# FFN tokens rounded to fp8 ahead of their transposition in a convolution, FFT and FFN block

## The chip, the cores and the metric

The kernel runs on one core of one Trainium2 chip. Times are device microseconds (us) of one execution. The core's engines are TensorE (PE, with its weight loads listed apart as PEld), VectorE (DVE), ScalarE (ACT), GpSimd (POOL) and SyncE (SP), which issues the loads and stores of the loop. The number that counts is the median time of the runs.

## The reference, cut to what matters

The input is 32 images of 56 x 56 pixels with 96 channels. Each image goes through three stages:

- a layer norm over channels, a linear map to 192 channels, a 3 x 3 convolution back to 96, silu, and the input added;
- a token mixer: layer norm, a linear map to 192 with relu, a Fourier transform over the 3136 tokens, a pointwise complex gate, the inverse transform and a linear map back to 96, added to the tokens;
- a feed-forward network (FFN): layer norm, then two linear layers (96 to 384 and back) whose factors are rounded to fp8 (5 exponent bits, 2 mantissa bits) and whose sums are rounded to fp16, with a relu between them, added to the tokens.

The change lies in the third stage. Its core in the reference:

```python
q_mul = lambda x: _float_quantize(x, 5, 2)
q_acc = lambda x: _float_quantize(x, 5, 10)
def _qlinear(x, W, b):
    y = q_acc(jnp.einsum('bsk,nk->bsn', q_mul(x), q_mul(W)))
    return q_acc(y + q_mul(b))
h = jax.nn.relu(_qlinear(x, W1, b1))
y = _qlinear(h, W2, b2)
...
t = t + ffn(_ln_t(t))
```

So the normalised tokens are rounded to fp8 before the first product.

## The kernel before, in words

An image's 3136 tokens lie as 112 partitions by 28 token columns (`N1`, `N2`) of 96 channels. The token columns are handled in 7 groups of 4 (`NG`, `G4`); the statistics and the convolution take chunks of 8, 8, 8 and 4 columns (`LN_CHUNKS`).

The convolution's input is made by products with a constant matrix (`image`, L153), its sums by the products of `conv` (L164, into `cv`); `to_tokens` (L196) transposes its result back. The mixer takes groups through `to_channels` (kind `n2`), `product_a` (L209, `ph`), `transform_a` (L218, `pa`), then a store of `u` to `da` in DRAM and a load of `at`, which turns the tokens round. `forward` (L233, `px`) does the second half of the transform from `at`; the gate follows on ScalarE and VectorE; `product_w2` (L272 and L276, `pg`) and `inverse` (L286, `pe`) lead to a second round trip through DRAM (`de`, then `y`), and `transform_out` (L294, `py`) ends the mixer.

The FFN of a group runs in these steps. `normal` (L479 to L488) makes the tokens `xn` from `t` on VectorE, one `tensor_scalar` for each token column with mean and reciprocal deviation as pointer operands; its output is f32, in a slot of the tag `xn` with two slots, which one load of image 0 shares (L362). `ffn_start` calls `ffn_tokens` (L297), which calls `to_channels` (L141): four TensorE transposes against the f32 identity (L146) put channels on the partitions, in the one PSUM buffer of the tag `tp`, which the mixer's `n2` transposes share. ScalarE's copy to `n3t` (L300) moves them out of PSUM and rounds them to fp8. `ffn_in` (L305, `pf`) multiplies by the first weights, three times a group, with an fp16 copy on ScalarE (L307). `ffn_relu` (L315, L316) works on VectorE, and `ffn_out` (L322, `po`) does twelve products a group with `hq` as weights. Over the 32 images the FFN has 224 groups and 896 transposes of `xn`.

The order of the work: `plan` gives each step of each image a due time by hand, in units of which an image has 8; images overlap by these times, so that the convolution of a coming image, the mixer and the FFN of earlier ones mix. `normal` is due at 0.7 and 0.55 before its group's FFN time, `ffn_start` at 0.35 before it, then three `ffn_first` and `ffn_middle`, `ffn_second` and `ffn_end`:

```python
put(at - 0.7, normal, g, 0)
put(at - 0.55, normal, g, 2)
put(at - 0.35, ffn_start, g)
```

`run` traces the steps in that order. The program framework then schedules the instructions itself, by priority and an estimate of time that it keeps as it goes (`schedule_with_timeline_sim=True`, L848), sets the semaphores, and assigns buffers. An engine's final order can therefore differ from the traced one within a short distance: products of other steps stand between the transposes of one group in places.[...]

At the start, `make_identity` (L89) builds the f32 identity on GpSimd, and a setup section prepares weights on VectorE and TensorE (L617, L675 and L719 are instructions of it), while the first tokens are loaded.

Of the kernel before, what the change touches and what calls it, by code (L numbers as in the profile page):

```python
# [38 lines left out]
F32 = mybir.dt.float32  # L39
F16 = mybir.dt.float16  # L40
F8 = mybir.dt.float8e5
AF = mybir.ActivationFunctionType
ALU = mybir.AluOpType
AX = mybir.AxisListType

C = 96
HW = 56
N = HW * HW
N1, N2 = 112, 28
# [9 lines left out]
G4 = 4  # L59
# [21 lines left out]
def hybrid_kernel(ctx: ExitStack, tc: tile.TileContext, x, par, spar, w_in, conv_w, w1, w2, fw1, fb1, fw2, fb2, fa, fb, ib, ia, rows6, out):  # L81
    nc = tc.nc
    nb = x.shape[0]

    const = ctx.enter_context(tc.tile_pool(name="const", bufs=1))


    ident = const.tile([128, 128], F32, name="ident")
    make_identity(nc, ident)  # L89
    mhalf = const.tile([N1, N2], F32, name="mhalf")  # L90
    nc.gpsimd.memset(mhalf, -0.5)

# [26 lines left out]
    xnp = ctx.enter_context(tc.tile_pool(name="xnp", bufs=2))  # L119
# [21 lines left out]
    def to_channels(xs, b, g, kind):  # L141

        rows = xs.shape[2]
        ps = psum.tile([rows, G4, N1], F32, tag="tp", name=f"tp_{kind}_{b}_{g}")
        for j in range(G4):
            nc.tensor.transpose(ps[:, j, :], xs[:, j, :], ident[:N1, :N1])  # L146
        return ps

    def image(xa, n, b, j0):
# [49 lines left out]
    def channels(xs, b, g):  # L199
        ps = to_channels(xs, b, g, "n2")  # L200
        n2t = w3.tile([C + 1, G4, N1], F32, tag="n2t", name=f"n2t_{b}_{g}")
        nc.scalar.copy(n2t, ps)
        return n2t
# [93 lines left out]
    def ffn_tokens(xs, b, g):  # L297
        ps = to_channels(xs, b, g, "n3")
        n3t = work.tile([C, G4 * N1], F8, tag="n3t", name=f"n3t_{b}_{g}")
        nc.scalar.copy(n3t, ps.rearrange("c j p -> c (j p)"), saturate=False)  # L300
        return n3t
# [177 lines left out]
    def normal(im, g, j):  # L479

        i = g // 2
        if j == 0:
            im.xc[g] = xnp.tile([N1, G4, C], F32, tag="xn", name=f"xn_{im.b}_{g}")
        mu, _, rs = im.norm[i]
        xc = im.xc[g]
        for j in (j, j + 1):
            at = g % 2 * G4 + j
            nc.vector.tensor_scalar(xc[:, j], im.t[i][:, at, :C], mu[:, at : at + 1], rs[:, at : at + 1], ALU.subtract, ALU.mult)  # L488

    def ffn_start(im, g):  # L490
        im.held["n3", g] = ffn_tokens(im.xc.pop(g), im.b, g)
# [27 lines left out]
    def plan(b):  # L519
# [27 lines left out]
        for g in range(NG):  # L547
            at = FIRST + g
            put(at - 0.35, tokens_a, g)
            for j2 in range(2):  # L550
                put(at + 0.15 + 0.6 * j2, forth, g, j2)
                put(at + 0.42 + 0.58 * j2, forth_a, g, j2)
            put(at + 1.2, store_a, g)
            at = BACK + g
            put(max(BACK - 0.6, at - 2.9), fetch_y, g)
            put(at, back, g)
            put(at + 0.15, back_end, g)
            at = FFN + g
# [3 lines that stand above are left out]
            for k in range(3):  # L562
                put(at + 0.28 * k, ffn_first, g, k)
                put(at + 0.28 * k + 0.17, ffn_middle, g, k)
            put(at + 1.0, ffn_second, g)
            put(at + 1.15, ffn_end, g)
            put(at + 1.5, store, g)
# [35 lines left out]
    with tc.tile_pool(name="setup", bufs=1) as sp, tc.tile_pool(  # L603
        name="setup_ps", bufs=2, space=bass.MemoryType.PSUM
# [15 lines left out]
        for g in range(2):  # L620
            ps = spp.tile([128, 512], F32, tag="ps", name=f"ps_wt{g}")
# [6 lines left out]
        for k in range(9):  # L628
            ps = spp.tile([128, 512], F32, tag="ps", name=f"ps_we{k}")
# [29 lines left out]
        for g in range(2):  # L659
            nc.vector.tensor_scalar(w1s[:, g, :C], w1s[:, g, :C], s1[:, g : g + 1], None, ALU.mult)  # L660
            nc.vector.tensor_copy(w1s[:, g, C : C + 1], o1[:, g : g + 1])
            ps = spp.tile([128, 512], F32, tag="ps", name=f"ps_w1{g}")
            nc.tensor.transpose(ps[: C + 1, :C], w1s[:, g, :], ident[:C, :C])
            nc.vector.tensor_copy(w1a[:, g * C : (g + 1) * C], ps[: C + 1, :C])
        ps = spp.tile([128, 512], F32, tag="ps", name="ps_w1c")
# [12 lines left out]
        for g in range(2):  # L678
            ps = spp.tile([128, 512], F32, tag="ps", name=f"ps_w2{g}")
# [6 lines left out]
        ps = spp.tile([128, 512], F32, tag="ps", name="ps_o2")  # L686
# [17 lines left out]
        for k in range(3):  # L704
            ps = spp.tile([128, 512], F32, tag="ps", name=f"ps_f1{k}")
            nc.tensor.transpose(ps[:C, :128], f1[:, k, :], ident)
            nc.vector.tensor_copy(w1q[:, k * 128 : (k + 1) * 128], ps[:C, :128], saturate=False)
            ps = spp.tile([128, 512], F32, tag="ps", name=f"ps_f2{k}")
# [143 lines left out]
```

## Time and profile before

| what | us |
|---|---|
| median of 3 runs | 3248.47 |
| lowest and highest of them | 3239.42, 3249.1 |
| profiled execution, its own time | 3247.36 |
| its span, first to last instruction | 3245.6 |
| TensorE busy | 3167.5 |
| TensorE weight loads busy | 2737.2 |
| VectorE busy | 2529.4 |
| ScalarE busy | 2196.2 |
| GpSimd busy | 598.2 |

The profile is one execution recorded by the hardware. An instruction group is given by its line, engine and operation, with output and inputs by name, then the tile as partitions by elements and type. For TensorE, `112*96 112x112` means 112 rows and 96 columns of weights, and 112 partitions by 112 elements streamed past them. After the count stand busy us and the mean ns of one, then the idle time before the group and what ended it. A wait line gives who waited for what, us in total, times, and the longest one. In a timeline each line is a start, a length, an engine and what ran, several like instructions merged into one line; an entry in square brackets is the idle time before it. The granted TensorE clock averaged 0.986 of full speed over the execution. The program spans stretches at the start and the end where only one or two images are at work; between them, images follow each other in a steady rhythm.

### The profile page before, as it was taken

Reading aid. Unit: us, or ns where it says so; the run is one execution under the profiler, and the core shown is the slowest. Engines: PE = TensorE matmul, PEld = TensorE weight load, DVE = VectorE, ACT = ScalarE, POOL = GpSimd, SP = SyncE. Lnnn points to the kernel's source line nnn. Section 1 sums busy time; section 2 is a strip of 40 time slices with the busy share of each in tenths; the row PEclk is TensorE's granted clock in tenths of the full one; section 3 lists DMA queues with packets and bytes.
Section 4 is the critical chain, followed back from the end, with each engine's and each line's share of the span. In section 5 each row is a group of like instructions: output and inputs, shape, how many; then the busy total and the mean of one; then the engine's idle time right before and its main releaser. Section 6 shows DMA issues by size and latency. Waiting matters only on the chain.

```text
span 3245.6 us, 66513 instructions
## 1 busy us (share of the span) xinstructions
PE 3167.5 (98%) x23701; PEld 2737.2 (84%) x23701; DVE 2529.4 (78%) x7829; ACT 2196.2 (68%) x5232; POOL 598.2 (18%) x397
## 2 busy tenths in 40 slices
PE   7999999999999999999999999999999999999997
PEld 6888888888888888888888888888888888888875
DVE  5557878877877877877877887878787878787777
ACT  2556676766776676766676766667667667767676
POOL 1211212111212111212121121111121112121111
PEclk8999999999999999999999999999999999999997
DMA  4343344343344433344333344333344333443341
GB/s 109 94 116 103 93 122 122 111 115 101 104 122 117 115 109 108 106 118 120 108 103 106 109 127 122 101 109 105 109 127 117 108 109 95 120 124 97 103 118 56
DMA packets 334551, 355.43 MB, mean 110 GB/s; under 512 B 129305, under 2 KB 287401, under 8 KB 333993
## 3 DMA queue, kind: packets, MB, share of 16 engines
q1 hardware_dynamic: 332210, 349.01, 38.6%
q8 instruction: 187, 3.06, 0.4%
q10 hardware_dynamic: 2008, 2.17, 0.2%
q14 instruction: 146, 1.19, 0.1%
HBM read 196.93 MB, written 154.14 MB: 108 GB/s over the span
## 4 chain that ended last, share of the span: by engine, by line
PE 87%; DMA 7%; DVE 3%; ACT 1%; issue 1%; SPq 0%; POOL 0%; ACTq 0%; DVEq 0%; POOLq 0%
PE cv L164 21%; PE px L233 9%; PE ph L209 9%; PE pa L218 8%; PE im L153 7%; PE tp_n L146 5%; PE pg L276 5%; PE pe L286 5%; PE pg L272 5%; PE py L294 4%; PE pf L305 4%; PE po L322 4%; DMA de<-es 2%; PE st L196 2%; DMA at<-da 2%; DMA y<-de 1%
## 5 line engine op out<-in xcount | busy, mean ns | idle before, releaser
L164 PE MATMUL cv<-img,wv 97*96 97x224 f32 (+1 forms) x4608 | 874.7, 330 | 0.2
L164 PEld LDWEIGHTS cv<-img,wv 97*96 97x96 f32 x4608 | 671.3, 164 | 101.0 <-issue 16.4
L138 POOL TENSOR_TENSOR rs_c<-var_c,mhalf 112x8 f32<-112x8 f32 (+1 forms) x128 | 198.3, 1549 | 1404.5 <-DVE var_c L136 1039.0
L307 ACT CAST h<-pf 128x448 f16<-128x448 f32 x672 | 362.2, 539 | 87.2 <-PE pf L305 86.4
L138 POOL TENSOR_TENSOR rs_b<-var_b,mhalf 112x8 f32<-112x8 f32 (+1 forms) x128 | 193.9, 1515 | 1194.7 <-DVE var_a L136 592.8
L233 PEld LDWEIGHTS px<-fb_sb,at 112*64 112x64 f32 (+1 forms) x3584 | 329.7, 165 | 94.7 <-issue 42.0
L212 ACT ACTIVATE h<-ph,rs_b 112x192 f32<-112x192 f32 x896 | 330.0, 424 | 105.7 <-PE ph L209 102.6
L233 PE MATMUL px<-fb_sb,at 112*64 112x112 f32 (+3 forms) x3584 | 378.2, 273 | 21.7 <-DMA at<-da 19.3
L209 PE MATMUL ph<-w1a,n2t 97*112 97x192 f32 x1792 | 380.2, 329 | 3.3 <-DVE sv L252 2.0
L218 PE MATMUL pa<-h,fa_sb 112*112 112x384 f32 x896 | 366.7, 491 | 0.3 <-DVE t L398 0.3
L315 DVE TENSOR_SCALAR h<-h,b1q 128x448 f16<-128x448 f16 x658 | 216.4, 329 | 178.1 <-ACT h L307 170.4
L153 PE MATMUL im<-rows_sb,xa 112*97 112x168 f32 x1792 | 333.4, 312 | 11.3 <-DVE xa L372 10.1
L209 PEld LDWEIGHTS ph<-w1a,n2t 97*112 97x112 f32 x1792 | 288.9, 177 | 32.1 <-DVE sv L252 2.6
L249 DVE SCALAR_TENSOR_TENSOR sv<-px,spar_sb,av 128x224 f32<-128x224 f32 (+2 forms) x352 | 153.9, 437 | 183.3 <-ACT av L240 180.7
L153 PEld LDWEIGHTS im<-rows_sb,xa 112*97 112x97 f32 x1792 | 262.9, 167 | 25.1 <-DVE xa L372 10.1
L219 ACT COPY u<-pa 112x384 f32<-112x384 f32 x448 | 216.2, 482 | 80.7 <-PE pa L218 76.3
L316 DVE CAST hq<-h 128x448 fp8e5<-128x448 f16 x672 | 259.2, 386 | 11.7 <-ACT h L313 6.7
L305 PE MATMUL pf<-n3t,w1q 96*128 96x448 fp8e5 x672 | 243.1, 362 | 7.4 <-ACT h L307 6.2
L276 PE MATMUL pg<-w2x,gt 128*112 128x96 f32 (+1 forms) x1792 | 245.3, 260 | 0.0
L322 PEld LDWEIGHTS <-hq 128*112 128x112 fp8e5 x2688 | 198.5, 135 | 51.7 <-DVE hq L316 16.9
L276 PEld LDWEIGHTS pg<-w2x,gt 128*112 128x112 f32 (+1 forms) x1792 | 239.8, 178 | 1.0
L488 DVE TENSOR_SCALAR xn<-t,st_c,rs_c 112x96 f32<-112x96 f32 x896 | 231.7, 324 | 10.1 <-POOL rs_c L138 7.3
(115 smaller groups left out, 6121.7 us busy)
## 6 DMA issues: line engine op xcount, KB each, us to landing
da<-u SPq DMA_DIRECT2D x224, 336.0 KB, 2.9
at<-da SPq DMA_DIRECT2D x224, 336.0 KB, 4.8
de<-es SPq DMA_DIRECT2D x448, 84.0 KB, 2.5
y<-de SPq DMA_DIRECT2D x224, 168.0 KB, 3.0
out<-o SPq DMA_DIRECT2D x224, 168.0 KB, 2.6
xl<-in_x SPq DMA_DIRECT2D x96, 336.0 KB, 3.5
x<-in_x SPq DMA_DIRECT2D x96, 336.0 KB, 4.0
xl<-in_x SPq DMA_DIRECT2D x32, 168.0 KB, 2.3
```

The costliest lines, as they stand in the source:

```text
L138: nc.gpsimd.tensor_tensor(rs, var, mhalf[:, :n], ALU.pow)
L153: nc.tensor.matmul(ps[:, j], xa[:, j, :], rows6_sb, start=True, stop=True)
L164: nc.tensor.matmul(ps[:, at], wv[:, k, dx, :], cols, start=(dx == 0), stop=(dx == 2))
L209: nc.tensor.matmul(ph[:, j, :], n2t[:, 2 * j2 + j, :], w1a, start=True, stop=True)
L212: nc.scalar.activation(h[:, j], ph[:, j], AF.Relu, scale=rs[:, 2 * j2 + j : 2 * j2 + j + 1])
L218: nc.tensor.matmul(pa, fa_sb, h, start=True, stop=True)
L233: nc.tensor.matmul(px[rows, j], lhs, fb_sb[:, first(p) : first(p + 1)], start=True, stop=True)
L276: nc.tensor.matmul(pg[:, half, j, :], lhs, w2x, start=False, stop=True, skip_group_check=True)
L305: nc.tensor.matmul(pf, w1q[:, k * 128 : (k + 1) * 128], n3t, start=True, stop=True)
L307: nc.scalar.copy(h1, pf)
L316: nc.vector.tensor_copy(hq[:, k, :], h2, saturate=False)
L322: nc.tensor.matmul(po[:, j, :], hq[:, k, j * N1 : (j + 1) * N1], w2q[:, k, :], start=(k == 0), stop=(k == 2))
```

## The change

The tokens are written as fp8 by `normal`, and the four transposes of a group are ordinary products of these fp8 tokens (as weights) with an fp8 identity. The result in PSUM is f32 as before, with values that are already rounded, and ScalarE's copy to `n3t` stays. The fp8 identity is made once at the start by VectorE from the f32 one. The mixer's transposes (`n2`) and the slots of the tags stay. Line numbers move by 2 from L90 on and by 5 from L147 on.

```diff
     ident = const.tile([128, 128], F32, name="ident")
     make_identity(nc, ident)
+    ident8 = const.tile([N1, N1], F8, name="ident8")
+    nc.vector.tensor_copy(ident8, ident[:N1, :N1], saturate=False)
...
         for j in range(G4):
-            nc.tensor.transpose(ps[:, j, :], xs[:, j, :], ident[:N1, :N1])
+            if xs.dtype == F8:
+                nc.tensor.matmul(ps[:, j, :], xs[:, j, :], ident8, start=True, stop=True)
+            else:
+                nc.tensor.transpose(ps[:, j, :], xs[:, j, :], ident[:N1, :N1])
         return ps
...
         if j == 0:
-            im.xc[g] = xnp.tile([N1, G4, C], F32, tag="xn", name=f"xn_{im.b}_{g}")
+            im.xc[g] = xnp.tile([N1, G4, C], F8, tag="xn", name=f"xn_{im.b}_{g}")
...
-            nc.vector.tensor_scalar(xc[:, j], im.t[i][:, at, :C], mu[:, at : at + 1], rs[:, at : at + 1], ALU.subtract, ALU.mult)
+            nc.vector.tensor_scalar(xc[:, j], im.t[i][:, at, :C], mu[:, at : at + 1], rs[:, at : at + 1], ALU.subtract, ALU.mult, saturate=False)
```

## The prediction

> **What bounds the kernel now.** I read the page's busy times and chain first, to name the engine, and then left the start and the end of the run aside and asked for the busy time and TensorE's waits of the stretch from 340 to 3140 us, in which one image takes the place of another every 97.8 us.
>
> ```profile
> PE 3167.5 (98%) x23701; PEld 2737.2 (84%) x23701; DVE 2529.4 (78%) x7829; ACT 2196.2 (68%) x5232; POOL 598.2 (18%) x397
> ...
> PE 87%; DMA 7%; DVE 3%; ACT 1%; issue 1%; SPq 0%; POOL 0%; ACTq 0%; DVEq 0%; POOLq 0%
> ```
>
> ```profile
> 340.00:3140.00 2800.00, 2773.16 (x21101) 2410.28 (x21100) 2235.73 (x6929) 1954.13 (x4673) 525.46 (x338) 1.00 0.40 111
> ```
>
> ```profile
> PE px L233 <- DMA at<-da: 16.9, 25, 2.7
> PE py L294 <- DMA y<-de: 5.8, 12, 1.3
> ```
>
> The second fence is the stretch (busy us of TensorE, its weight loads, VectorE, ScalarE, GpSimd; clock; DMA share); the third holds its two largest waits of TensorE (us in total, times, longest). TensorE is busy 2773 of 2800 us, at the full clock, and waits for other engines hardly at all: once an image for the transposed forward spectrum, less for the inverse one. But overlapping products make a busy share a poor measure, so the question is how densely they follow one another. A product's own duration says little there[...]; the distance from one start to the next is what it takes from TensorE.
>
> The groups of products by shape, then stretches of TensorE's timeline (start us, us, what):
>
> ```profile
> L305 PE MATMUL pf<-n3t,w1q 96*128 96x448 fp8e5 x672 | 243.1, 362 | 7.4 <-ACT h L307 6.2 <-DVE xn L488 0.6 <-ACT n3t L300 0.2
> L322 PE MATMUL po<-w2q,hq 128*112 128x96 fp8e5 x2688 | 215.7, 217 | 5.1 <-DVE hq L316 5.0
> L146 PE MATMUL tp_n<-ident,xn 112*96 112x112 f32 x896 | 152.7, 265 | 1.2 <-DVE xn L488 1.1
> ```
>
> ```profile
> 1600.63 0.92 PE L164 MATMUL cv<-img,wv 97*96 97x224 f32 x4
> 1601.39 0.81 PE L209 MATMUL ph<-w1a,n2t 97*112 97x192 f32 x4
> 1602.04 0.45 PE L153 MATMUL im<-rows_sb,xa 112*97 112x168 f32 x2
> ```
>
> ```profile
> 1615.10 0.67 PE L322 MATMUL po<-w2q,hq 128*112 128x96 fp8e5 x10
> 1615.61 0.87 PE L209 MATMUL ph<-w1a,n2t 97*112 97x192 f32 x4
> 1616.31 0.26 PE L164 MATMUL cv<-img,wv 97*96 97x112 f32 x1
> ```
>
> ```profile
> 1642.06 0.55 PE L146 MATMUL tp_n<-ident,xn 112*96 112x112 f32 x4
> 1642.44 0.73 PE L164 MATMUL cv<-img,wv 97*96 97x224 f32 x3
> ```
>
> ```profile
> 1619.89 0.26 PE L146 MATMUL tp_n<-ident,xn 112*96 112x112 f32 x1
> 1619.99 0.61 PE L233 MATMUL px<-fb_sb,at 112*128 112x112 f32 x4
> 1620.44 0.26 PE L146 MATMUL tp_n<-ident,xn 112*96 112x112 f32 x1
> 1620.53 0.39 PE L233 MATMUL px<-fb_sb,at 112*128 112x112 f32 x2
> ```
>
> Read the starts. Four f32 transposes of xn take 1642.44 - 1642.06 = 0.38 us, 95 ns each. Ten fp8 products of 96 columns take 1615.61 - 1615.10 = 0.51 us, 51 ns each. And the same four ph products take 0.65 us behind f32 work (1601.39 to 1602.04) but 0.70 us behind fp8 work (1615.61 to 1616.31): a short fp8 product hides too little of the f32 weight load that follows. The last fence shows the framework's scheduler laying other products between the four transposes of a group.
>
> [...]pf with 448 columns starts its follower 191 to 193 ns later[...]. For f32 the trace shows double: 323 ns for pa's 384 columns.[...]
>
> **The change, part by part.**
>
> *Transposes, the only part on TensorE.* 896 products (32 images x 7 groups x 4) go from f32 to fp8, both the moving identity (112 columns) and the weights (96). Now: median distance 96 ns. After: [...]51 measured on po, whose weights are larger and whose columns are fewer. I take 50. Gain 896 x 46 ns = 41.2 us, all on the path, since TensorE is the bound.
>
> *What the switch back costs.* Behind a po product, an f32 one with a load of 96 or 97 columns ends 42 ns later than behind f32 (im 186 against 143 ns from the end before; cv 231 against 189), one of 112 columns 55 ns later (ph 219 against 163). An fp8 transpose covers some 7 ns more than po (112 columns for 96): 35 and 48 ns; for 128 columns another 13 by the same step, so 61. How often it is paid depends on the runs. In TensorE's order the 896 transposes form 375 runs: 147 of one, 39 of two, 85 of three, 104 of four. 69 are followed by an fp8 product, which I set at nothing, 116 by an f32 one with 96 or 97 columns, 110 with 112, 80 with 128 (px, as in the last fence). Sum: 116 x 35 + 110 x 48 + 80 x 61 = 14.2 us. Net 27.0 us. The bounds: nothing is paid (41 us gained), or every transpose is followed by f32 work (896 x 47 = 42 us lost, gain nil).
>
> *VectorE, L488.* It writes the normalised tokens as fp8: the same 896 instructions.
>
> ```profile
> L488 DVE TENSOR_SCALAR xn<-t,st_c,rs_c x896: 299/324/339, 241.4 to 3220.9; 112x96 f32<-112x96 f32 x180
> ```
>
> ```profile
> 26.20 0.19 DVE L719 CAST b<-b 112x96 fp8e5<-112x96 f32 x1
> ```
>
> The first is its line (min/median/max ns), the second a cast of the same 96 elements from f32 to fp8 in the setup, 0.19 us: no slower than f32 to f32 of that size (L617 0.26 with one pointer operand). From L617 to L675, a like operation on 192 elements in 0.31 us, 96 more elements cost 0.05 us.[...] I take nothing. VectorE is idle for 3246 - 2529 = 716 us and TensorE waits 1.1 us for xn[...].
>
> *The rest.* The identity's cast at the start: one VectorE instruction, about 0.2 us by L719, in front of statistics that wait 3.6 us for the first load; nothing. The eviction L300 reads the same f32 PSUM tile and rounds values that are fp8 already: same cost. No DMA, no pool depth and no semaphore in the loop is added; the xn slots keep their f32 size, since a load of image 0 shares them. The eviction may begin about 0.18 us sooner after the group's first transpose (four times 46 ns), which helps.
>
> *What is late next.* With some 0.8 us less TensorE work an image, TensorE comes sooner to px and py, whose data makes a round trip through DRAM that doesn't shrink. These waits can grow by what is saved inside the round trip. The page's DMA part gives the landings as 2.9 us for da, 4.8 for at, 2.5 for de and 3.0 for y, together 13.2 of the 97.8 us of an image; the same share of 0.8 us is 0.11 us an image, 3.5 us in all. Forecast gain 27.0 - 3.5 = 23.5 us.
>
> The profiled execution took 3247.4 us (span 3245.6), the median of the runs is 3248.5: the two are 0.03% apart. 3247.4 - 23.5 = 3224 us.
>
> **The rivals.**
>
> *The gain comes whole.* If the scheduler keeps the groups of four together, 224 runs remain: 224 x 47 = 10.5 us of switches, gain 31; if fp8 neighbours hide those too, 41. That gives 3206 to 3217 us. For it: the order is made anew from changed instructions. Against it: the interleaving comes from due times and from when xn is ready, and both stay.
>
> *The switches eat it.* If the transposes are strewn singly among f32 products, or f32 loads stall behind fp8 more than po shows, the gain is 0 to 9 us: 3238 to 3247, within 0.3% of the time now, which is about what a measurement of this kernel can tell from no change. 147 single transposes speak for it, the 104 whole groups against. That the change doesn't do what it says belongs here: would the fp8 product keep the f32 pace, the time would stay.
>
> *A new order opens a wait: slower.* The scheduler orders the instructions by its own running estimate of time, and cheaper transposes shift that estimate at each of 224 groups. One mechanism, one place: px L233 reaches `at` before the round trip has landed. Its wait is 16.9 us in 25 times now, 0.7 each, and 2.7 at the longest. Were it at the longest in all 32 images, 32 x 2.7 = 86 us, 69 more than now; less the 23.5, that is 46 slower, 3293 us. It decides from 23.5 / 32 = 0.73 us more an image; half of the 69 gives 3258. For it: this is TensorE's largest wait. Against it: px is placed by hand, and its fetch isn't touched.
>
> **How the numbers follow.** Forecast 0.48 (3217 to 3238); the gain whole 0.12; eaten 0.22; slower 0.18. Faster by over 0.3% is the sum of the first two, 0.60. The range runs from 3205, just under the whole gain, to 3262, which takes in the milder part of the slower case and leaves out about 0.1 there.
>
> **What would show it.** In the changed profile the L149 transposes should start some 50 ns apart in a run, and an f32 product behind one should end 35 to 60 ns late. The normalisation should stay near 324 ns with an fp8 output, the waits of px and py near 17 and 6 us between 340 and 3140 us, and an image near 97 us. Transposes still 95 ns apart, or many more runs than 375, would make the forecast too high a gain; a px wait above 40 us would make its sign wrong.

## The result, and the profile after

The changed kernel takes 3258.02 us (median of 20 runs, 3248.12 to 3263.27) against 3247.94 us (20 runs) of the kernel before beside it: a ratio of 1.0032 [1.0023, 1.0041]. It is slower by 10 us, where 23.5 us less were forecast. The profiled execution took 3260.1 us (span 3258.3).

First the page's busy times and its chain, as they were read of before.

```profile
PE 3163.0 (97%) x23701; PEld 2709.5 (83%) x23701; DVE 2522.8 (77%) x7830; ACT 2182.5 (67%) x5232; POOL 599.5 (18%) x397
...
PE 79%; DMA 9%; DVE 6%; ACT 3%; issue 1%; POOL 1%; SPq 0%; ACTq 0%; DVEq 0%; POOLq 0%
```

TensorE is busy 4.5 us less, although 41 us of transposing were to go, and its share of the chain fell from 87% to 79%: VectorE and the DMA now stand in the chain where TensorE stood. Next the transposes by shape and the line of the normalisation (min, median, max ns).

```profile
L149 PE MATMUL tp_n<-ident,xn 112*96 112x112 fp8e5 x896 | 99.6, 216 | 0.3 <-DVE xn L493 0.2
```

```profile
L493 DVE TENSOR_SCALAR xn<-t,st_c,rs_c x896: 297/323/371, 244.1 to 3233.8; 112x96 fp8e5<-112x96 f32 x180
```

Both did what was forecast. Within a run the fp8 transposes start 49 ns apart (the median of 578), and the part of TensorE's time that they add, taken as the distances from each end to the one before, fell from 98.9 to 51.4 us. The normalisation takes 323 ns instead of 324. So the loss lies elsewhere. The stretch from 340 to 3140 us, with the columns of before, and its waits of TensorE:

```profile
340.00:3140.00 2800.00, 2760.96 (x20994) 2375.57 (x20993) 2221.05 (x6897) 1929.55 (x4648) 524.70 (x336) 1.00 0.39 110
```

```profile
PE py L299 <- DMA y<-de: 13.4, 18, 2.0
PE ph L214 <- DVE t L479: 11.7, 5, 2.8
PE px L238 <- DMA at<-da: 8.0, 13, 1.1
```

In the same 2800 us only 20,994 products were done, where before it were 21,101. The px wait, where the prediction had set its slower case, fell from 16.9 to 8.0 us. A wait that wasn't in the list before has come: ph for VectorE's addition at L479 (L474 before), five times, 2.8 us at the longest. Here is the third of them. From the timeline (start us, length, engine, what; idle time ahead of it in brackets):

```profile
1507.11 0.96 DVE L377 TENSOR_TENSOR xa<-xl,rs_a 112x768 f32<-112x768 f32 x1 [0.99 <-POOL rs_a L140]
...
1508.10 1.86 SPq L369 DMA_DIRECT2D xl<-in_x  x2
...
1509.07 0.55 DVE L377 TENSOR_TENSOR xa<-xl,rs_a 112x384 f32<-112x384 f32 x1
...
1512.12 0.26 PE L327 MATMUL po<-w2q,hq 128*112 128x96 fp8e5 x2
...
1513.53 1.15 DVE L134 BATCH_NORM_STATS2 st_a<-xl 112x6 f32<-112x192 f32 x4 [1.10 <-DMA xl<-in_x]
1514.59 0.54 DVE L479 TENSOR_TENSOR t<-py,t 112x384 f32<-112x384 f32 x1
...
1515.19 1.62 PE L214 MATMUL ph<-w1a,n2t 97*112 97x192 f32 x4 [2.81 <-DVE t L479]
```

Read it from the end. TensorE's last product before the gap is po at 1512.12; ph needs the PSUM buffer (tag `c`) that L479 empties. L479's last py product had ended at 1510.79, but L479 stands in VectorE's queue behind the statistics L134 of a coming image, and these wait for that image's loads `xl`. The SPq line holds two loads. SyncE could issue the first only at 1508.10, when the first L377 shown had read one of the three `xl` buffers, and the second, for which L134 waits at 1513.53, only at 1509.64, when the second L377 had read another. So a load that has no place in TensorE's work at all holds TensorE for 2.8 us, through two engines and two pools. It happens in every fifth image, at about 530, 1023, 1515, 2010 and 2507 us.

Every fifth, because the order of the work is a new one. Between the two builds, 10,961 of TensorE's 14,880 instructions, as the kernel's code issues them, and 5,152 of VectorE's 7,829 stand at another place. Before, all images in the middle of the run had the same sequence on TensorE (from an image's first `im` product to that of the next one); now five sequences come by turns.

### The profile page after: what moved, and what is told of

Read it like the earlier page. It is cut to its first block, busy times and chain, and to the rows that moved or that the text cites. A ratio compares the mean times of both kernels' runs of the same rounds, so it can differ in the third digit from the quotient of the medians.

```text
span 3258.3 us, 66565 instructions
## 1 busy us (share of the span) xinstructions
PE 3163.0 (97%) x23701; PEld 2709.5 (83%) x23701; DVE 2522.8 (77%) x7830; ACT 2182.5 (67%) x5232; POOL 599.5 (18%) x397
## 4 chain that ended last, share of the span: by engine, by line
PE 79%; DMA 9%; DVE 6%; ACT 3%; issue 1%; POOL 1%; SPq 0%; ACTq 0%; DVEq 0%; POOLq 0%
PE cv L169 20%; PE px L238 8%; PE ph L214 8%; PE pa L223 8%; PE im L158 6%; PE pe L291 5%; PE pg L281 5%; PE pg L277 4%; PE py L299 4%; PE po L327 3%; PE pf L310 3%; DMA xl<-in_x 3%; DMA de<-es 3%; PE tp_n L151 2%; PE st L201 2%; DMA y<-de 1%
## 5 line engine op out<-in xcount | busy, mean ns | idle before, releaser
L140 POOL TENSOR_TENSOR rs_c<-var_c,mhalf 112x8 f32<-112x8 f32 (+1 forms) x128 | 193.8, 1514 | 1297.0 <-DVE var_c L138 976.7
L238 PE MATMUL px<-fb_sb,at 112*64 112x112 f32 (+3 forms) x3584 | 389.7, 275 | 13.5 <-DMA at<-da 12.6
L214 PE MATMUL ph<-w1a,n2t 97*112 97x192 f32 x1792 | 376.2, 329 | 14.1 <-DVE t L479 11.7
L158 PE MATMUL im<-rows_sb,xa 112*97 112x168 f32 x1792 | 335.6, 314 | 11.2 <-DVE xa L377 9.9
L321 DVE CAST hq<-h 128x448 fp8e5<-128x448 f16 x672 | 257.8, 384 | 11.2 <-ACT h L318 5.9
L493 DVE TENSOR_SCALAR xn<-t,st_c,rs_c 112x96 fp8e5<-112x96 f32 x896 | 233.3, 322 | 36.0 <-POOL rs_c L140 35.6
L281 PE MATMUL pg<-w2x,gt 128*112 128x96 f32 (+1 forms) x1792 | 252.4, 261 | 0.0
L243 ACT ACTIVATE av<-px,spar_sb 128x224 f32<-128x224 f32 (+2 forms) x352 | 155.3, 441 | 138.3 <-PE px L238 128.8
```

Source lines behind the costliest of these rows:

```text
L140: nc.gpsimd.tensor_tensor(rs, var, mhalf[:, :n], ALU.pow)
L158: nc.tensor.matmul(ps[:, j], xa[:, j, :], rows6_sb, start=True, stop=True)
L214: nc.tensor.matmul(ph[:, j, :], n2t[:, 2 * j2 + j, :], w1a, start=True, stop=True)
L238: nc.tensor.matmul(px[rows, j], lhs, fb_sb[:, first(p) : first(p + 1)], start=True, stop=True)
L281: nc.tensor.matmul(pg[:, half, j, :], lhs, w2x, start=False, stop=True, skip_group_check=True)
L321: nc.vector.tensor_copy(hq[:, k, :], h2, saturate=False)
```

## The experiments

Most of them force an order. The program is built once for its order alone, with the products of one variant; then it is built again with the products and buffers that are to run, and each engine's instructions are tied to that recorded order by edges that carry no wait:

```diff
+    _, _, order = trace(ORDER_OF_FP8, None, ())
+    nc, feed, said = trace(PRODUCTS_IN_FP8, order, ENGINES)
...
+                for engine in engines:
+                    mine = traced[engine]
+                    for a, b in zip(order[engine], order[engine][1:]):
+                        tc.add_manual_dep(mine[b], mine[a].name, info, reason="order")
```

Below, "old order" is that of the kernel before and "new order" that of the changed one. In these kernels the lines are other ones: ph L189, px L213, py L274 to L276.

### Products and order apart

**e1**: the changed products in the old order (`ORDER_OF_FP8, PRODUCTS_IN_FP8 = False, True`, all five engines).

> The changed kernel, but every engine issues its instructions in the order of the kernel before (the scheduler is bound to that order; only the cast of the identity is extra). Theory A (the products are cheap as forecast, and the loss comes from the new order): the forecast gain appears, 3214 to 3232 us, 16 to 33 under the kernel before. Rival B (fp8 products cost TensorE something beyond their pace and the switch, whatever the order): about as slow as the changed kernel, 3250 to 3265 us. Rival C (the other engines take back whatever TensorE saves): 3240 to 3250 us, like the kernel before.

Measured: 3231.27 us, ratio 0.9949 [0.9935, 0.9963].

**e2**: the old f32 products in the new order (`True, False`).

> The kernel before (f32 transposes), but every engine issues in the order of the changed kernel. Theory A (the order makes the loss): slower than the changed kernel by about the products' gain, 3280 to 3295 us. Rival B (fp8 products make the loss): near the kernel before, 3243 to 3253 us. Rival C: between them, about the changed kernel's 3258 us, since the waits would take up the difference.

Measured: 3282.95 us, ratio 1.0115 [1.0102, 1.0128].

So the change is two changes. The products alone gain 15 us, the order alone loses 37 us; together they lost 10. (The two don't add up: in the new order the products gain more. The part on the prediction comes back to this.) **e5** and **e6** ask which engine's order it is: in e5 TensorE alone has the old order (`ENGINES` holds it alone), in e6 the other four have it and TensorE is left to the scheduler.

> The changed kernel with TensorE alone bound to the order of the kernel before; the other engines are scheduled freely around it. If the loss lies in TensorE's own order (split groups, products that ran side by side no longer adjacent), the whole 27 us come back: about 3231 us, as when all engines had the old order. If it lies in the order of the other engines, VectorE above all, much of it stays: 3242 to 3258 us.

> The changed kernel with VectorE, ScalarE, GpSimd and SyncE bound to the order of the kernel before, and TensorE scheduled freely around them. If the loss is a queue effect on the other engines (VectorE blocked behind a load or a GpSimd result while TensorE waits for an eviction): 3228 to 3238 us. If it is TensorE's own order: 3245 to 3260 us.

Measured: e5 3232.23 us, ratio 0.9958 [0.9944, 0.9973]; e6 3244.16 us, 0.9995 [0.9987, 1.0003]. TensorE's old order alone brings back all that e1 did; the other engines' order alone brings back less than half.

**e3** and **e4** move the due times of `normal` a little earlier, before and after the change, to see whether any new order costs that much:

```diff
-            put(at - 0.7, normal, g, 0)
-            put(at - 0.55, normal, g, 2)
+            put(at - 0.75, normal, g, 0)
+            put(at - 0.6, normal, g, 2)
```

> The kernel before, with the two due times of the normalisation 0.05 earlier, so that the scheduler lays out another order for the same work. Theory A needs that order alone can move the time by some tenths of a per cent: 3235 to 3275 us, away from the kernel before by 5 us or more. Against it: within 3 us of the kernel before.

> The changed kernel, with the same nudge of 0.05 to the due times of the normalisation. Theory A: another order for the same cheaper products, so a time away from the changed kernel by 5 us or more, anywhere from 3220 to 3275 us. Rival B: within 3 us of the changed kernel's 3258.

Measured: e3 3249.01 us, 1.0006 [0.9997, 1.0016]; e4 3255.66 us, 1.0033 [1.0021, 1.0045]. This says nothing of other orders, for the nudge changed none: in the trace of e3 TensorE and VectorE have, instruction by instruction, the order of the kernel before, and in that of e4 the order of the changed kernel. The two are repeats, and e4 shows the changed kernel 9 us slower than the kernel before on the chip of e1 and e2 too.

### The late load

**e7** keeps the changed products and the new order on every engine and gives `xl` a fourth buffer. To make room, `y2` of the FFN has one buffer instead of two, and image 0's last load no longer borrows a slot of `xn`:

```diff
-        tag, bufs = ("xn", 2) if im.b == 0 and i == 3 else ("xl", 3)
+        tag, bufs = "xl", 4
...
-        y2 = work.tile([N1, G4, C], F16, tag="y2", name=f"y2_{b}_{g}")
+        y2 = work.tile([N1, G4, C], F16, tag="y2", bufs=1, name=f"y2_{b}_{g}")
```

> The changed kernel's order on every engine, but four buffers in place of three for the prefetched input chunks xl, so that a load needn't wait until the multiply of an older chunk has freed its buffer (y2 gets one buffer instead of two to make room; both of its instructions are on VectorE). If VectorE blocked on the late load, with TensorE's ph behind it, is a main part of the loss: VectorE's wait for xl falls from 60 us to under 20 between 340 and 3140 us, TensorE's ph wait for the py eviction from 12 us to under 3, and the time to 3238 to 3250 us. If it is a side show: 3253 to 3260 us.

Measured: 3230.25 us, ratio 0.9948 [0.9931, 0.9964]. Its waits of TensorE from 340 to 3140 us:

```profile
PE py L274 <- DMA y<-de: 13.8, 17, 1.7
PE px L213 <- DMA at<-da: 8.0, 10, 2.5
PE ph L189 <- DVE t L454: 2.6, 3, 0.9
```

The ph wait fell from 11.7 to 2.6 us, the others stayed, and 25 us came off (14.7 us under the kernel before on its chip, where the changed kernel is 10.1 above it): more than expected. VectorE's own wait for `xl` fell too, from 60.2 to 25.5 us, less far than expected. As the extra gain could be worth as much in any order, three controls followed: **e9** (f32 products, old order, four buffers), **e10** (fp8, old order, four) and **e12** (f32, new order, four). In e9 and e12 `sd` of the convolution has one buffer as well.

> Control: the kernel before in its own order on every engine, with four xl buffers (y2 and sd get one buffer instead of two; both are written and read on VectorE alone). If the late load is a fault of the new order, nothing is to be had here: 3241 to 3248 us. If a fourth buffer helps any order, 15 to 28 us come off, 3217 to 3231 us, and the finding on the new order is no explanation of the change's loss.

> fp8 products in the order of the kernel before on every engine, with four xl buffers. If the old order has no late load to cure, as the first experiment without the buffer: 3226 to 3234 us. If loads and cheaper products add up, 3205 to 3220 us.

> f32 transposes in the order of the changed kernel on every engine, with four xl buffers (y2 and sd in one). If the new order's loss of 37 us with f32 transposes is the late load as well, some 28 us of it come back, 3250 to 3260 us, and TensorE's ph wait for the py eviction falls under 3 us. If the load's share hangs on TensorE being faster, less than 12 us come back: over 3270 us.

Measured: e9 3235.38 us, 0.9969 [0.9958, 0.998]; e10 3217.3 us, 0.9912 [0.9896, 0.9928]; e12 3258.55 us, 1.0039 [1.0025, 1.0054]. The fourth buffer helps the old order as well. All eight medians, and in brackets the difference to the kernel before on the same chip (it stood between 3244.9 and 3247.9 us on the chips used):

| us | 3 load buffers | 4 load buffers |
|---|---|---|
| f32, old order | 3246.4 (before) | 3235.4 (e9, -11.2) |
| f32, new order | 3283.0 (e2, +36.6) | 3258.6 (e12, +12.0) |
| fp8, old order | 3231.3 (e1, -15.1) | 3217.3 (e10, -29.3) |
| fp8, new order | 3258.0 (after, +10.1) | 3230.3 (e7, -14.7) |

With fp8 products the new order costs 25 us with three load buffers (10.1 + 15.1) and 15 with four (29.3 - 14.7). The late load is thus worth some 11 of the 25; with f32 products the same sum gives 13 of 37. By resampling the runs, a difference between two of these kernels is uncertain by 5 to 8 us, and the 11 by some 10. Part of what the buffer gains has nothing to do with the late load of the middle: at the same product of TensorE's order, e7, e10 and e12 are already 3 to 5 us ahead of their three-buffer kernels 150 us after the start. Which of the edit's parts does this was not tried. **e11** is the same edit on the changed kernel with the scheduler left free, the two-line diff above and nothing else:

> The changed kernel as it stands, with four xl buffers and y2 in one, and the scheduler free to lay out its own order with them. If the fourth buffer is a cure that doesn't hang on one order: 3225 to 3240 us. If the scheduler takes the buffer into account and lays out another order with waits of its own: 3240 to 3262 us.

Measured: 3234.93 us, ratio 0.9964 [0.995, 0.9979], 11.6 us under the kernel before. That is the expected cure, but not yet a gain of the fp8 tokens: the f32 products in their old order with the same four buffers (e9) are 11.2 us under it. The scheduler's order in e11 is a third one, and the 29.3 us of e10 show what the products and the buffer give together in the old order. A freely scheduled f32 kernel with four buffers was not run.

### The other half: a group of products cut in two

In all new-order runs so far px with 64 columns of weights took TensorE longer: 98.3 us of busy time, where the old order has 85.8. From the timelines of TensorE, first of the kernel before, then of the changed one:

```profile
1529.60 0.99 PE L233 MATMUL px<-fb_sb,at 112*64 112x112 f32 x16
1530.51 0.30 PE L146 MATMUL tp_n<-ident,xn 112*96 112x112 f32 x1
```

```profile
1537.77 0.79 PE L238 MATMUL px<-fb_sb,at 112*64 112x112 f32 x10
1538.49 0.36 PE L310 MATMUL pf<-n3t,w1q 96*128 96x448 fp8e5 x1
1538.78 0.60 PE L238 MATMUL px<-fb_sb,at 112*64 112x112 f32 x6
1539.31 1.00 PE L169 MATMUL cv<-img,wv 97*96 97x224 f32 x4
```

A whole group takes 0.91 us from its start to the next product. Cut by a pf product it takes 1.54, of which 0.29 pass from the start of pf to the next piece: 0.34 us are lost. The products of a group write the two halves of the PSUM partitions by turns (`slice(64 * half, 64 * half + 64)`). A group is 8 or 4 products in the code, twice as many instructions in the profile. In the trace of the whole group the instructions start in pairs: two of them 7 ns apart and, from the second pair on, the next two 96 ns later. That makes 57 ns an instruction (0.91 / 16), against the 95 of f32 transposes of the same 112 columns. The cut leaves five products of the code in one piece and three in the other, and the last two instructions of either piece start singly, 96 ns apart (at 1538.20 and 1538.30, at 1539.03 and 1539.12). The old order has its 128 groups in 138 pieces, the new one in 184.

**e13** and **e14** have the new order on every engine, but put each such group together again in TensorE's order, at the place of its last product, with four and with three load buffers:

```diff
+    def together(order, groups):
+        place = {k: i for i, k in enumerate(order)}
+        move = {}
+        for g in groups:
+            at = max(place[k] for k in g)
+            for k in g:
+                move[k] = at
+        return sorted(order, key=lambda k: (move.get(k, place[k]), place[k] if k not in move else k))
```

> The changed products, the new order on every engine and four load buffers (3230 us so far), but in TensorE's order the 16 products of a 64-column px group, which the new order strews, are put together at the place of the last of them. Theory: the halves of such a group run side by side only when they alternate without other products between them; the traces show some 10 us of overlap lost in the new order, so the time falls to 3220 (3217 to 3224) and TensorE's busy time for the 64-column px of 112 columns from about 98 to 86 us. Rival: the lost overlap is covered by other products and the rest of the new order's loss is scattered waits: 3228 to 3233.

> The same with the three load buffers of the changed kernel (3258 us so far). Theory: the same 10 us come off, 3248 (3244 to 3252), and the ph wait for VectorE's add stays near 12 us. Rival: 3255 to 3260.

Measured: e13 3214.17 us, ratio 0.9899 [0.9883, 0.9915]; e14 3241.84 us, 0.9984 [0.9975, 0.9992]. Either is some 16 us under the same kernel with cut groups (e7 3230.3; after 3258.0), more than the expected 10. The busy time of these products, before, after and in e14:

```profile
L233 PE MATMUL px<-fb_sb,at 112*64 112x112 f32 x1280 | 85.8, 267 | 0.0
```

```profile
L238 PE MATMUL px<-fb_sb,at 112*64 112x112 f32 x1280 | 98.3, 270 | 0.0
```

```profile
L213 PE MATMUL px<-fb_sb,at 112*64 112x112 f32 x1280 | 82.5, 267 | 0.0
```

From after to e14 it fell by 15.8 us, about all of the gain. All 128 groups are whole now, so there are 56 pieces fewer than in the changed kernel (184 - 128), ten of which the old order has too; 15.8 us over 56 are 0.28 us a cut, near the 0.34 of the one shown. And in e14 the ph wait stayed, 13.3 us in five times, so the two halves of the loss are separate.

### The switch back to f32, and the px wait

**e15** takes e10 (fp8, old order, four load buffers) and puts the four transposes of each group together in the same way: 224 runs instead of 375.

> The changed products, the old order and four load buffers (3217 us so far), with the four fp8 transposes of each group put together in TensorE's order, at the place of the last of them: 224 runs instead of 375. Theory: each run of fp8 transposes costs one late start of the f32 product behind it, 35 to 48 ns, so 151 runs fewer save some 6 us: 3211 (3208 to 3214). Rival: holding the first transposes back to the last makes ScalarE's copy and the products behind it late, or a switch is hidden by other work: 3216 to 3225.

Measured: 3208.39 us, ratio 0.9885 [0.9863, 0.9907]; 8.9 us under e10. The busy time of the transposes in e10, then in e15:

```profile
L124 PE MATMUL tp_n<-ident,xn 112*96 112x112 fp8e5 x896 | 110.0, 217 | 1.3 <-DVE xn L468 1.3
```

```profile
L124 PE MATMUL tp_n<-ident,xn 112*96 112x112 fp8e5 x896 | 83.4, 215 | 1.1 <-DVE xn L469 1.1
```

8.9 us by 151 runs are 59 ns a run, and the result speaks against the rival, that holding transposes back makes others late; with five and six runs, though, the difference is uncertain by some 8 us. The busy time falls by far more than the time does, since products overlap: taken as the distances from each end to the one before, the transposes add 56.3 us in e10 and 51.3 in e15.

**e8** asks whether the px wait eats part of the gain in the old order. It is e1, with the first px of an image due later, and with an order laid out anew (with f32 products) from these due times:

```diff
-                at += 2 * m + (0.14 if m + u == 0 else 0)
+                at += 2 * m + (0.26 if m + u == 0 else 0)
```

> fp8 products in an order made with f32 transposes, as in the first experiment, but from due times in which the first px of an image comes 0.12 of a unit (some 1.5 us) later. TensorE's px wait grew from 17 to 29 us when the old order got cheaper transposes. If that wait is what took the forecast gain down from 23 to 15 us, the later px gives 8 to 12 us back: 3219 to 3225 us. If the wait only moves on, or the new order opens others: 3228 to 3245 us.

Measured: 3247.17 us, ratio 1.0005 [0.9998, 1.0011], 16 us slower than e1. TensorE's waits in e1, then in e8:

```profile
PE px L213 <- DMA at<-da: 29.1, 29, 2.8
PE py L274 <- DMA y<-de: 6.0, 13, 1.7
```

```profile
PE py L274 <- DMA y<-de: 23.7, 16, 2.3
PE st L176 <- ACT s L171: 14.1, 26, 1.0
PE px L213 <- DMA at<-da: 0.6, 1, 0.6
```

The px wait is gone and two others have taken its place. The expectation is missed: here the due time moved by hand sent the wait on and didn't remove it. As e8 has an order of its own, it also says something that e3 and e4 could not: with the same products and three load buffers, the five orders of e1, e5, e6, e8 and the changed kernel took 3231, 3232, 3244, 3247 and 3258 us.

## Why the prediction was wrong, by its own steps

Two steps failed. That the order of the work stays made the sign wrong; the price of what is late next was too small even in the old order.

- **Transposes: right.** 50 ns were taken, the author's estimate next to po's 51; 49 were measured between starts; 47.5 us less of TensorE's time by ends, forecast 41.2 (43.0 less in e1, in the old order).
- **Normalisation, eviction, identity at nothing: right.** 323 ns against 324 for the normalisation, 532 against 528 for ScalarE's copy to `n3t` (medians), one cast of 0.26 us for the identity; VectorE's busy time fell by 6.6 us.
- **The switch back: right in kind and in size.** Its 35, 48 and 61 ns were estimates, from the 42 and 55 measured behind po and pf's pace (193 ns for 448 columns, 7 for 16). The weight loads of before agree with the reading: ahead of the first ph behind po (1615.61) the load takes 178 ns and starts 43 ns before the product, ahead of the first ph behind cv (1601.39) it takes 176 and starts 188 before. After an fp8 transpose the followers end late by 35 ns (cv and im), 48 (ph, pa) and 46 (px, where 61 was taken); of the frequent ones only st, with 5, is cheaper. Over all 375 runs of the old order the followers end 14.8 us later in e1 than before, and 15.0 later in e10 than in e9; 14.2 were forecast. With 43 us saved on the transposes themselves, TensorE's own net is 28 us, forecast 27.0. The 59 ns a run of e15 are more than this switch: 5 of its 8.9 us lie in the transposes' own ends, much of it where a run begins behind 64-column px. There the first transpose ends 180 ns after the px, elsewhere about 50; e15 has 30 such places, e10 59.
- **What is late next: the right place, the wrong size.** 3.5 us were taken for px and py together. Between 340 and 3140 us these two waits grew from 22.7 us before to 35.1 in e1, and with four buffers from 20.5 in e9 to 29.5 in e10:

```profile
PE px L213 <- DMA at<-da: 14.7, 20, 3.5
PE py L274 <- DMA y<-de: 5.8, 11, 1.4
```

```profile
PE px L213 <- DMA at<-da: 22.5, 29, 3.1
PE py L274 <- DMA y<-de: 7.0, 13, 2.1
```

The net of 28 us less 12.4 and 9.0 is 16 and 19; measured were 15.1 (e1) and 18.1 (e9 to e10), so the sum closes. (The profiled execution of e1 was 8 us over its median, so its wait may be on the high side.)
- **The order stays: this step failed.** The prediction held that "the interleaving comes from due times and from when xn is ready, and both stay". It doesn't stay: with fp8 products in place of 896 f32 ones the scheduler laid out most places of TensorE's and VectorE's queues anew. The runs of transposes became even fewer (318 for 375), as the rival of the whole gain had hoped. But with the fp8 products the new order cost 25 us. Some 11 are the late load (e1, e7, e10, after). Whole px groups give back 16 to 18 us (e7 and e13, after and e14), of which 46 of the 56 cuts, 13 to 15 us, are the new order's own. The two make up the 25 within the noise, and with both mended the new order (e13, 33.1 us under the kernel before) is no slower than the old one (e10, 29.3); the 4 us between them are not clear of noise.
- **The slower rival: the right mechanism in the wrong place.** "A new order opens a wait" is half of what happened, but it named px, whose wait fell to 8 us, and no rival named the cut groups. That it gives 3258 us for half of its wait, the time that was measured, is luck. The case was priced by the largest wait of before; the wait that came was one which before had shown nothing on TensorE's list. A trace of before did hold a hint: VectorE waited 39.4 us for `xl` in 48 times. In the changed kernel it is 60.2, as the line of VectorE's waits shows:

```profile
DVE st_a L134 <- DMA xl<-in_x: 60.2, 60, 2.4
```

Such a wait was counted as harmless, since VectorE has 716 us to spare. Here it wasn't: L479, queued behind it, frees a PSUM buffer, and ph waited 11.7 us for that.

The same accounts say why the products gain more in the new order (some 26 us, from e2 to after and from e12 to e7) than in the old (15 and 18). With 318 runs the followers lose 12 us instead of 15, so the net is 31; and TensorE's waits for px, py and ph together grow by only 2 us (31.0 to 33.1 from e2 to after). What stays open is where a fourth buffer gains 11 us for the kernel before, on whose list of TensorE's waits the late load doesn't show.

## What to carry to other kernels

Where a scheduler orders the instructions by its own estimate of time, a cheaper instruction can also be a new order; build both orders, compare them, and measure products and order apart before judging the edit. Then look for two things that such an order can break and no engine's total busy time shows: a wait of an idle engine that stands in its queue ahead of an instruction which frees the busy engine's buffer (11.7 us of ph here), and a group of products that is cut in two (some 0.28 us a cut of a 64-column px group here). And compare with the same buffers on both sides: a buffer more on the load was worth 11 us to the kernel before and 25 to the changed order, as much as the edit itself.

## What the runs showed of the hardware that was not expected

Behind its longest gaps TensorE ran at a clock of half for 3.4 or 6.8 us. The columns of these stretches of the changed kernel, around the gap shown above, are those of the long stretch (the third from the end is the granted clock):

```profile
1508.00:1514.00 6.00, 4.38 (x40) 3.26 (x39) 4.26 (x14) 4.21 (x10) 0.05 (x1) 1.00 0.68 196
1514.00:1521.00 7.00, 5.81 (x24) 5.74 (x25) 5.04 (x17) 2.50 (x7) 1.64 (x1) 0.52 0.38 127
1521.00:1545.00 24.00, 24.00 (x185) 20.61 (x184) 16.18 (x55) 16.36 (x41) 2.70 (x2) 1.00 0.41 116
```

The gap began at 1512.4; from about 1514 to 1521 the clock was halved (0.52 in the second stretch), and TensorE did 24 products where the third stretch has 54 in 7 us (185 in 24). The clock column read in half-microsecond steps, the halved spells last 3.4 us or 6.8. In the changed kernel four lie between 340 and 3130 us, 20.5 us in all, each at the end of or behind one of the four ph gaps of 2.4 to 2.8 us; the fifth gap, at 1021 us, was 1.1 us long and had none. In the kernel before there is none in this stretch. Less the 1.8 us that fall into the gaps, half of the 20.5 is, as an estimate, some 9 us of work lost, beside the 11.7 us of the gaps themselves. The granted clocks of the single runs agree: from the 20 runs of the changed kernel (mean 0.9856, some 94 us at half the clock) to the 6 of e7 (0.9885, 74 us) it is 20 us less. Over those 20 runs (3248 us at 0.988 to 3263 at 0.984) each us at half the clock goes with 0.4 us more time. So, as an estimate, some 8 of the 25 us that the fourth buffer gains are the clock's, and 9 are the wait of ph itself. The length of the gap alone doesn't settle what follows. In the changed kernel the four gaps of 2.4 to 2.8 us had a halved clock 1.8 to 3.5 us after their start; its other gaps in this stretch, up to 2.0 us (the longest at 2196 us), and those of the kernel before, up to 1.7, had none. But in e1 a gap of some 1.7 us at 2756 us and one of 1.5 at 3050 were each followed by 3.4 us at half the clock, another of 1.7 at 2861 wasn't, and in e10 one of 2.1 at 2841 wasn't either.
